# Layer 1 of a two-layer graph attention network: the tile's last two neighbouring multiplied rows are added on GpSimd first

## The chip, the cores and the metric

The kernel runs on one core of a Trainium2 chip. The metric is the device time of one execution in microseconds (us), from the first to the last instruction and what lies around them. Each execution computes the whole network from inputs in HBM. The engines are TensorE (PE, its weight loads PEld), VectorE (DVE), ScalarE (ACT), GpSimd (POOL) and SyncE (SP, which only issues DMAs here). Each engine works through its own list of instructions in order; semaphores hold an instruction until what it needs is done.

## What is computed

Two graph attention layers with a residual and a layer norm each, over 10000 nodes with 768 features and 170000 edges (self loops among them); the reference adds one more self loop to each node. All in float32. Cut to what matters for layer 1 (4 heads of 256 columns, 1024 in all):

```python
src, dst = ei[0], ei[1]
xl = (x @ W).reshape(n, heads, out_ch)
alpha_src = einsum('nhc,hc->nh', xl, a_src)
alpha_dst = einsum('nhc,hc->nh', xl, a_dst)
e = leaky_relu(alpha_src[src] + alpha_dst[dst], 0.2)
e = exp(e - segment_max(e, dst)[dst])
alpha = e / (segment_sum(e, dst)[dst] + 1e-16)
h = segment_sum(xl[src] * alpha[:, :, None], dst)   # the sum of this case
h = relu(layer_norm(h + b1)) + (x @ Wr1 + br1)
# layer 2 the same with one head of 768 columns, then
# x = layer_norm(x + layer 2 + its residual)
```

## The kernel before

**Stages.** First a table is made (to about 900 us): for each tile of 128 nodes `x @ W1` and the attention terms are written to a table in HBM, while the edges are sorted into lists. Then layer 1 runs (`ordered_layer1`, about 910 to 3350 us), then layer 2 (to the end).

**Tiles of layer 1.** The nodes are sorted by degree and cut into 79 tiles of 128 nodes, one node a partition. A tile `t` has `n = SLOTS[t]` rows: row `k` holds, for each of its 128 nodes, the table row of the node's k-th neighbour (1033 floats a partition). `n` goes from 8 up to 41 in the middle tile and down to 9; there are 1377 rows in all. The rows come by GpSimd's indirect DMAs (`gather`, L426) into a ring of 29 rows in SBUF (`Ring`, `RING1 = 29`). `ring.fetch(upto)` issues all gathers below `upto` that are not issued yet; it is called after each row, so the gather that reuses a row's place is queued on GpSimd right after the row was used, and waits for that use.

**The weighted sum of a tile** is made in `acc`, which lies in PSUM, from three kinds of rows:

- the first `on_pe(t)` rows (1 to 4) go through TensorE: ScalarE writes diagonal matrices of the weights (L725), TensorE multiplies the rows by them into `acc` (L731). In tiles of 22 rows and more, the later groups have such rows too;
- of the rest every fourth (`SHARE = 4`) is weighted by VectorE alone, `acc += weight * row`, four instructions of 256 columns (`weigh`, L531);
- all others are `shared`: ScalarE multiplies the row in place by its weights (`multiply`, L520, four instructions), `LEAD = 3` rows ahead in the program's order, and VectorE adds the whole row to `acc` (`weigh`, L527, one instruction of 1024 columns).

VectorE takes the rows in order, so `acc` is read and written by one instruction after the other.

**The next tile's weights** are prepared by VectorE in between. Before row `n - 3` it makes the logits of the next tile: L489 adds the attention terms in the ring's rows to `ad`, L190 is the leaky relu, L493 the largest, L496 the subtraction (about 1.05 us in all); ScalarE takes the exponential (L497). Before row `n - 2` VectorE normalises them: L514, L508, L509, L510, L511 (about 1.2 us). Then ScalarE writes the diagonals and TensorE starts the next tile's rows. In the text below the first of these is called the list step and the second the normalising step. All operands of both lie in SBUF. On GpSimd each list step has a few short instructions as well (L500, L501).

**The end of a tile** on VectorE is the layer norm: L542 and L544, L556, L558, L856 (about 5.7 us); its first weighted row of the next tile then waits until TensorE's L731 is complete. TensorE's order in a tile is: transposes of x (L697), transposes of `h` (L697), `x @ Wr1` (L173, 24 matmuls), the layer-2 table row (L879, 32 matmuls), then L731 of the next tile.

The schedule is written out by hand: each engine executes in the order in which the Python emits.

Of the kernel before, what the change touches and what calls it, by code (L numbers as in the profile page):

```python
# [48 lines left out]
LEAD = 3  # L49
# [3 lines left out]
ON_PE1 = 4  # L53
PARTED2 = 26
PARTED = 22


def chunk_counts(n_edges):
# [23 lines left out]
def gnn_kernel(ctx, tc, x, x_cols, src, dst, src_col, dst_col, W1, a_src1, a_dst1, b1, g1, be1, Wr1, br1,  # L82
               W2, a_src2, a_dst2, b2, g2, be2, Wr2, br2, out, n_edges):
    nc = tc.nc
    N, D0 = out.shape
    H1, DH1 = a_src1.shape
    H2, DH2 = a_src2.shape
    C1, C2 = H1 * DH1, H2 * DH2
# [8 lines left out]
    SLOTS = CAPS  # L97
# [3 lines left out]
    FIRST, TOTAL = [0] * NT, 0  # L101
# [420 lines left out]
    def weigh(acc, row, e, dh, first=None, shared=False):  # L522


        if shared:
            c = e.shape[1] * dh
            nc.vector.tensor_add(acc[:, :c], acc[:, :c], row[:, :c])  # L527
            return
        for h in range(e.shape[1]):
            s = slice(h * dh, (h + 1) * dh)  # L530
            nc.vector.scalar_tensor_tensor(acc[:, s], row[:, s], e[:, h:h + 1],  # L531
                                           (acc if first is None else first)[:, s], op0=OP.mult, op1=OP.add)
# [110 lines left out]
    SLOTS, FIRST = [SLOTS[t] for t in TURNS], [FIRST[t] for t in TURNS]  # L643
# [31 lines left out]
    def ordered_layer1(mem):  # L675
        nc.scalar.add_instruction(mybir.InstLoadActFuncSet(name=nc.get_next_instruction_name(), act_func_set_id=6, engine=nc.scalar.engine))
        with tc.tile_pool(name="b1", bufs=1) as pool, tc.tile_pool(name="small1", bufs=2) as small, \
# [3 lines left out]
            ring = Ring(table1, RING1, {}, [mem.rearrange("p (k n) -> p k n", n=R1)])  # L681
# [30 lines left out]
            def on_pe(t):  # L712


                return min(max(SLOTS[t] // 2 - 5, 1), ON_PE1, SLOTS[t])

            def later_on_pe(t):

                return min(max((SLOTS[t] - 20) // 2, 1), ON_PE1)
# [61 lines left out]
            def cuts_of(t):  # L781

                n = SLOTS[t]
                groups = 1 if n < PARTED else -(-2 * n // ring.size)
                size = 8 if groups == 2 else (n - 5) // groups
                return [0] + [n - size * g for g in range(groups - 1, -1, -1)]

            def by_vector(t, k):
                lo = max(c for c in cuts_of(t)[:-1] if c <= k)
                return k - lo >= (later_on_pe(t) if lo else on_pe(t))  # L790

            def shared(t, k):
                return by_vector(t, k) and (k - on_pe(t)) % SHARE > 0

            last = None
            full = None
            ready = []
# [18 lines left out]
            for t in range(NT + 1):  # L816
                live, events = t < NT, []
                n = SLOTS[t] if live else 0
                first = done = on_pe(t) if live else 0
                cuts = cuts_of(t) if live else []  # L820
                if live and not ready:
# [3 lines left out]
                def row_of(k):  # L825
                    lo = max(c for c in es if c <= k)
                    return es[lo][0][:, k - lo], es[lo][1] if k == lo else None

                def multiplied(upto):
                    nonlocal done  # L830
                    while done < min(upto, n):
                        if shared(t, done):
                            multiply(ring.slot(FIRST[t] + done), row_of(done)[0], DH1)
                        done += 1
# [5 lines left out]
                if live:  # L840
                    es, acc = ready
# [52 lines left out]
                def due(k):  # L894
                    while events and events[0][0] <= k:
                        events.pop(0)[1]()
# [5 lines left out]
                for k in range(n):  # L902
                    if k + 2 * LEAD + 2 in cuts[1:-1]:
                        next(later)
                    if k + 2 * LEAD in cuts[1:-1]:
                        lo, es_lo = next(later)
                        es[lo] = es_lo
                    multiplied(k + 1 + LEAD)
                    if n - LEAD <= k < n - LEAD + 2:
                        ready += itertools.islice(ahead, 1)  # L910
                    if k + 2 in cuts[1:-1]:
                        next(later)
                    weights, fade = row_of(k)
                    if fade is not None:
                        for h in range(H1):
                            s = slice(h * DH1, (h + 1) * DH1)
                            nc.vector.scalar_tensor_tensor(acc[:, s], acc[:, s], fade[:, h:h + 1], ring.slot(FIRST[t] + k)[:, s],
                                                           op0=OP.mult, op1=OP.add)
                    if by_vector(t, k):
                        weigh(acc, ring.slot(FIRST[t] + k), weights, DH1, shared=shared(t, k))  # L920
                    ring.fetch(FIRST[t] + k + 1 + ring.size)
                    due(k)
                due(DEGREES)
                ready += itertools.islice(ahead, max(2 - len(ready), 0))
# [409 lines left out]
    with tc.If(all_fits > 0) as fit:  # L1334
        with tc.tile_pool(name="rows", bufs=1) as rows_pool:
            mem = rows_pool.tile([P, RING1 * R1], F32, name="ring")
            ordered_layer2(mem, ordered_layer1(mem))
# [49 lines left out]
```

## Time and profile before

| | us |
|---|---|
| median of 3 runs | 5521.68 |
| lowest and highest | 5516.3 and 5529.82 |
| the profiled execution | 5544.64 |
| its span, first to last instruction | 5542.8 |
| busy in the span: PE, DVE | 4908.0, 4286.7 |
| busy in the span: ACT, POOL | 2828.9, 3296.8 |
| in layer 1: 807 adds of a shared row (L527) | 993.8 |
| in layer 1: 1248 weighted quarter rows (L531) | 610.9 |
| in layer 1: 1361 gathers on POOL (L426) | 1389.0 |

The last three are from the groups of instructions between 913 and 3350 us. The profile has one record of each instruction: engine, line, start, duration, and what ended the idle time before it. "a<-b,c" names what is written and what is read. Busy time is not a bound by itself: which engine sets the pace has to be read from the waits of each stage.

### The profile page before, as it was taken

To read this page: it belongs to the slowest core of one execution; us is meant where nothing else is said; L and a number is where in the kernel's file an instruction comes from. 1 tells how busy PE (TensorE), PEld (TensorE's weight loads), DVE (VectorE), ACT (ScalarE), POOL (GpSimd) and SP (SyncE) were. 2 spreads that over 40 slices of the span, in tenths; PEclk is the share of its full clock that TensorE was granted. 3 is DMA by queue.
4 is the path that set the end of the run, shared out by engine and by line. 5 is a ranking of instruction groups with operands and counts; after the bars stand their busy time and mean duration, and the time that the engine had idled before them with its cause. 6 is when DMAs were issued, how large, how long until landed. Compare 5 with 4: busy or idle time off the path is not lost. (4 is left out here: it accounts for less than half of the span.)

```text
span 5542.8 us, 60338 instructions
## 1 busy us (share of the span) xinstructions
PE 4908.0 (89%) x15304; PEld 2913.5 (53%) x15307; DVE 4286.7 (77%) x7678; ACT 2828.9 (51%) x8248; POOL 3296.8 (59%) x3429
## 2 busy tenths in 40 slices
PE   8999996999999887889999997999888887877765
PEld 3444443555555555555655554666555555555544
DVE  5883244899998888899999995988777776766776
ACT  3434343777778788778777772332322222222222
POOL 2446365556666666666666544666665665666663
PEclk9999997999999999999999998999998988888887
DMA  4333626899999998999999977999988888888885
GB/s 156 122 96 88 94 91 236 312 344 354 363 376 363 356 348 292 342 348 369 374 365 358 341 272 263 333 331 333 329 313 286 301 304 291 291 290 289 298 291 184
DMA packets 474313, 1591.43 MB, mean 287 GB/s; under 512 B 118328, under 2 KB 122488, under 8 KB 473959
## 3 DMA queue, kind: packets, MB, share of 16 engines
q0 software_dynamic: 322384, 1286.62, 65.5%
q1 hardware_dynamic: 149520, 297.43, 16.1%
q10 hardware_dynamic: 2054, 3.42, 0.2%
q8 instruction: 129, 2.11, 0.2%
q14 instruction: 226, 1.84, 0.1%
HBM read 1431.80 MB, written 177.29 MB: 290 GB/s over the span
## 5 line engine op out<-in xcount | busy, mean ns | idle before, releaser
L426 POOL DMA_INDIRECT ring<-table,slots x2675 | 2658.3, 994 | 1633.8 <-issue 616.4
L531 DVE SCALAR_TENSOR_TENSOR acc<-ring,e,acc 128x256 f32<-128x256 f32 (+1 forms) x2546 | 1586.7, 623 | 141.6 <-PE acc L731 44.0
L520 ACT ACTIVATE ring<-ring,e 128x256 f32<-128x256 f32 x3232 | 1320.8, 508 | 1.4 <-issue 1.3
L527 DVE TENSOR_TENSOR acc<-acc,ring 128x1024 f32<-128x1024 f32 x808 | 995.1, 1232 | 78.1 <-remote 5.5
L1033 PE MATMUL big<-wr,w 128*128 128x512 f32 (+1 forms) x2464 | 875.8, 501 | 142.1 <-issue 138.2
L988 PE MATMUL big<-ring,diagonals 128*128 128x256 f32 x2754 | 750.4, 431 | 197.5 <-issue 149.1
L173 PE MATMUL big<-w,xT 128*128 128x512 f32 x1896 | 824.7, 597 | 26.3 <-DMA w<-in_W_dram 9.8
L173 PE MATMUL big<-wr,xT 128*128 128x512 f32 x1896 | 832.6, 596 | 0.2 <-ACT xT L698 0.2
L879 PE MATMUL half<-w,hT 128*128 128x512 f32 (+1 forms) x2528 | 830.5, 486 | 0.0
L988 PEld LDWEIGHTS big<-ring,diagonals 128*128 128x128 f32 x2754 | 590.4, 218 | 360.9 <-issue 226.9
L1033 PEld LDWEIGHTS big<-wr,w 128*128 128x128 f32 x2464 | 482.2, 196 | 503.6 <-issue 471.9
L987 ACT ACTIVATE diagonals<-ident,e 128x128 f32<-128x128 f32 x1377 | 423.1, 388 | 609.8 <-remote 228.6
L879 PEld LDWEIGHTS half<-w,hT 128*128 128x128 f32 x2528 | 477.7, 189 | 367.8 <-issue 330.8
L731 PE MATMUL acc<-ring,diagonals 128*128 128x256 f32 x2056 | 514.3, 406 | 138.2 <-ACT diagonals L725 99.5
L173 PEld LDWEIGHTS big<-w,xT 128*128 128x128 f32 x1896 | 361.7, 191 | 484.9 <-issue 466.9
L173 PEld LDWEIGHTS big<-wr,xT 128*128 128x128 f32 x1896 | 356.4, 191 | 419.9 <-issue 419.2
L731 PEld LDWEIGHTS acc<-ring,diagonals 128*128 128x128 f32 x2056 | 411.0, 203 | 237.8 <-ACT diagonals L725 125.2
L546 ACT ACTIVATE sd<-mv,eps 128x1 f32<-128x1 f32 x237 | 69.3, 292 | 690.2 <-DVE mv L544 426.5
L725 ACT ACTIVATE diagonals<-ident,e 128x128 f32<-128x128 f32 x1028 | 315.4, 388 | 173.2 <-DVE e L511 115.8
L630 DVE TENSOR_TENSOR scr<-big,ad_b 128x1024 f32<-128x1024 f32 x79 | 96.7, 1225 | 377.5 <-ACT row L627 337.7
L635 POOL TENSOR_TENSOR row<-row,none 128x1024 f32<-128x1024 f32 x79 | 187.2, 2369 | 264.0 <-ACT row L627 261.4
L633 ACT ACTIVATE scr<-scr 128x256 f32<-128x256 f32 x632 | 253.5, 402 | 120.3 <-DVE scr L630 120.3
(185 smaller groups left out, 3453.5 us busy)
## 6 DMA issues: line engine op xcount, KB each, us to landing
ring<-table,slots POOLq DMA_INDIRECT x2675
table<-row SPq DMA_DIRECT2D x79, 516.0 KB
h_d<-hT SPq DMA_DIRECT2D x79, 512.0 KB
w<-h_d SPq DMA_DIRECT2D x77, 512.0 KB
table<-row SPq DMA_DIRECT2D x79, 385.0 KB
ring<-table SPq DMA_DIRECT2D x79, 385.0 KB
xT<-in_x_cols_dram SPq DMA_DIRECT2D x79, 384.0 KB
x_d<-xt SPq DMA_DIRECT2D x79, 384.0 KB
```

The costliest lines, as they stand in the source:

```text
L173: nc.tensor.matmul(p[:, c:e], aT[:, j, :], w[:, j, c:e], start=(j == 0), stop=(j == k - 1))
L426: nc.gpsimd.indirect_dma_start(out=to, out_offset=None, in_=table, in_offset=bass.IndirectOffsetOnAxis(ap=index, axis=0), **more)
L520: nc.scalar.activation(row[:, s], row[:, s], AF.Copy, scale=e[:, h:h + 1])
L527: nc.vector.tensor_add(acc[:, :c], acc[:, :c], row[:, :c])
L531: nc.vector.scalar_tensor_tensor(acc[:, s], row[:, s], e[:, h:h + 1], (acc if first is None else first)[:, s], op0=OP.mult, op1=OP.add)
L633: nc.scalar.activation(m[:, s], m[:, s], AF.Copy, accum_out=row[:, C1 + i * H1 + h:C1 + i * H1 + h + 1])
L725: nc.scalar.activation(diagonals[:, k * H1 + i, :], ident, AF.Copy, scale=e[:, k, i:i + 1])
L731: nc.tensor.matmul(acc[:, c:d], diagonals[:, k * H1 + i, :], ring.slot(q + k)[:, c:d], start=(k == 0 and c % BANK == 0), stop=(k == m - 1 ...
L879: nc.tensor.matmul(q, hT[:, j, :], w2[:, j, c:c + q.shape[1]], start=(j == 0), stop=(j == K1 - 1))
L987: nc.scalar.activation(diagonals[:, (k - lo) % G, :], ident, AF.Copy, scale=e[:, k - lo, :])
L988: nc.tensor.matmul(to, diagonals[:, (k - lo) % G, :], ring.slot(at + k)[:, ON_PE2:C2], start=False, stop=(k == n - 1), skip_group_check=True)
L1033: nc.tensor.matmul(r[:, c:d], hT[:, j, :], wr2[:, j, c:d], start=False, stop=(j == K1 - 1 and d < C2), skip_group_check=True)
```

## The change

In tiles of at least 14 rows two neighbouring shared rows, `pair` and `pair + 1`, the last such two in the tile's last group, are not added to `acc` one by one. GpSimd adds the first to the second in place in the ring, and VectorE adds that sum to `acc` as the tile's last row. The fetches that reuse the places of row `pair` and all later rows of the tile are put off to the tile's end.

```diff
+PAIRED = 14
...
+            def pair_of(t):
+
+                n, lo = SLOTS[t], cuts_of(t)[-2]
+                for k in range(n - 2 if n >= PAIRED else -1, lo, -1):
+                    if shared(t, k) and shared(t, k + 1):
+                        return k
+                return n
...
+                pair = pair_of(t) if live else 0
...
+                    if k == max(pair + 1 - LEAD, n - 5) and pair < n:
+                        one, two = (ring.slot(FIRST[t] + pair + j)[:, :C1] for j in (0, 1))
+                        nc.gpsimd.tensor_add(two, two, one)
                     weights, fade = row_of(k)
...
-                    if by_vector(t, k):
+                    if by_vector(t, k) and k not in (pair, pair + 1):
                         weigh(acc, ring.slot(FIRST[t] + k), weights, DH1, shared=shared(t, k))
-                    ring.fetch(FIRST[t] + k + 1 + ring.size)
+                    if pair < n and k == n - 1:
+                        weigh(acc, ring.slot(FIRST[t] + pair + 1), weights, DH1, shared=True)
+                        pair = n
+                    ring.fetch(FIRST[t] + min(k + 1, pair) + ring.size)
                     due(k)
```

By the code, 65 of the 79 tiles have a pair. Rows are numbered from 0; the list step stands before row n - 3, the normalising step before row n - 2. GpSimd's add is queued after the gather that follows the row in the third column:

| rows n | tiles | last row before the add | pair | order on VectorE from there, after the change |
|---|---|---|---|---|
| 14 | 6 | 9 | 12, 13 | row 10, list, 11, normalise, sum |
| 15 | 8 | 9 | 12, 13 | 10, 11, list, normalise, 14, sum |
| 16 | 7 | 10 | 13, 14 | 11, 12, list, normalise, 15, sum |
| 17 | 8 | 11 | 13, 14 | 12, list, normalise, 15, 16, sum |
| 18 | 7 | 12 | 14, 15 | 13, list, normalise, 16, 17, sum |
| 19 | 7 | 14 | 17, 18 | 15, list, 16, normalise, sum |
| 20 | 6 | 15 | 18, 19 | 16, list, 17, normalise, sum |
| 21 | 4 | 15 | 18, 19 | 16, 17, list, normalise, 20, sum |
| 22 | 4 | 16 | 18, 19 | 17, list, normalise, 20, 21, sum |
| 23 | 2 | 18 | 21, 22 | 19, list, 20, normalise, sum |
| 24 to 41 | 6 | | | as one or the other of these |

## The prediction

> **What bounds layer 1 now.** I read the groups of instructions first, for the prices of the two adds: VectorE's add of a shared row into PSUM, and the only large add that GpSimd does in this kernel, of the same size, in the table stage. The number after the bar is busy us, the next the mean ns of one.
>
> ```profile
> L527 DVE TENSOR_TENSOR acc<-acc,ring 128x1024 f32<-128x1024 f32 x808 | 995.1, 1232 | 78.1 <-remote 5.5
> L635 POOL TENSOR_TENSOR row<-row,none 128x1024 f32<-128x1024 f32 x79 | 187.2, 2369 | 264.0 <-ACT row L627 261.4
> ```
>
> Next the busy time by windows, cut at tile borders (from one L542 to the next): tiles of 15, 16, 17 and 19 rows. Columns: window, length, then busy us of PE, PEld, DVE, ACT and POOL, clock, DMA.
>
> ```profile
> 1226.20:1253.90 27.70, 25.91 (x88) 15.17 (x87) 25.83 (x41) 20.02 (x53) 16.76 (x20) 1.00 0.95 348
> 1337.00:1365.00 28.00, 27.54 (x96) 16.57 (x95) 26.02 (x41) 21.30 (x57) 17.75 (x21) 1.00 0.99 369
> 1451.50:1480.60 29.10, 27.78 (x95) 16.46 (x95) 27.11 (x42) 22.79 (x61) 19.40 (x20) 1.00 0.99 369
> 1631.40:1662.60 31.20, 29.85 (x104) 17.98 (x103) 28.55 (x43) 25.55 (x70) 21.60 (x25) 1.00 1.00 379
> ```
>
> Two engines are full at once. VectorE's missing 2 us are gaps of some 0.05 us between its 40 instructions; TensorE misses 0.5 us (16 rows) to 1.8 us (15). GpSimd has 8 to 11 us free. So VectorE's row is worth its 1.25 us only where TensorE leaves room for it, and from 19 rows on there is a third limit, seen in the timeline of one 19-row tile (start, duration; VectorE, then GpSimd, ScalarE, TensorE):
>
> ```profile
> 1653.37 2.57 DVE L527 TENSOR_TENSOR acc<-acc,ring 128x1024 f32<-128x1024 f32 x2
> 1655.85 0.30 DVE L489 TENSOR_TENSOR e<-ring 128x4 f32<-128x4 f32 x2
> 1656.18 0.30 DVE L190 SCALAR_TENSOR_TENSOR e<-e 128x76 f32<-128x76 f32 x1
> 1656.84 0.24 DVE L496 TENSOR_TENSOR e<-e,new 128x76 f32<-128x76 f32 x1
> 1656.99 2.06 DVE L531 SCALAR_TENSOR_TENSOR acc<-ring,e,acc 128x256 f32<-128x256 f32 x4
> 1659.96 0.24 DVE L511 TENSOR_TENSOR e<-e,total 128x76 f32<-128x76 f32 x1
> 1660.11 2.49 DVE L527 TENSOR_TENSOR acc<-acc,ring 128x1024 f32<-128x1024 f32 x2
> ```
>
> ```profile
> 1654.88 0.99 POOL L426 DMA_INDIRECT ring<-table,slots  x1 [0.35 <-issue]
> 1656.21 0.99 POOL L426 DMA_INDIRECT ring<-table,slots  x1 [0.34 <-issue]
> ```
>
> ```profile
> 1660.29 2.44 ACT L725 ACTIVATE diagonals<-ident,e 128x128 f32<-128x128 f32 x8 [2.91 <-DVE e L511]
> 1660.74 3.72 PE L731 MATMUL acc<-ring,diagonals 128*128 128x256 f32 x16 [0.26 <-ACT diagonals L725]
> ```
>
> The list step (L489 to L496) leads through the normalising step (to L511) and the diagonals to TensorE, which waits for them, and VectorE waits for TensorE at its next first row: in the waits of this tile DVE L531 <- PE L731 is 0.6 us, PE L731 <- ACT L725 0.9 us. So from 19 rows on the list step is on the path that sets the tile's length, and the rows after L511 (the two of 1660.11, which are the pair here) are not. GpSimd is in step with VectorE: its gather starts 0.27 us after the row before it ended (1654.61, the first of the two L527).
>
> **The part that hurts.** GpSimd's add falls exactly there. Last, a place where such an add met VectorE, in the table stage: the answer for L278, VectorE's short add with both inputs in SBUF, and the timeline where it met L635; then L630, VectorE's product with one input in PSUM, which runs beside L635 all the time.
>
> ```profile
> L278 DVE TENSOR_TENSOR before<-before,hot x79: 182/192/2272, 382.9 to 408.9; 128x64 bf16<-128x64 bf16 x79
> 382.94 2.38 POOL L635 TENSOR_TENSOR row<-row,none 128x1024 f32<-128x1024 f32 x1 [7.93 <-ACT row L627]
> 382.91 3.36 DVE L278 TENSOR_TENSOR before<-before,hot 128x64 bf16<-128x64 bf16 x6
> L630 DVE TENSOR_TENSOR scr<-big,ad_b x79: 1212/1225/1226, 24.1 to 877.9; 128x1024 f32<-128x1024 f32 x79
> ```
>
> Minimum, median and maximum in ns: 192 as a rule, 2272 at worst. Six of them at 382.91 took 3.36 us instead of 1.35: one was held until the GpSimd add had ended. It happened in both of the two places where an L278 started under an L635. L630 never went over 1226.
>
> **The change, part by part.** *VectorE's add removed*: 65 tiles with one L527 less, 1.25 us with its gap: 65 x 1.25 = 81 us at most. *ScalarE's multiplications*: unchanged. *Fetches put off*: the gathers for the last 2 to 4 places of a tile are issued at its end instead; the next tile's rows (n' of them) need places up to row n + n' - 30 of this one, which is below the pair in every tile, and GpSimd's free 8 to 11 us take them: 0; if that cover were gone, the list step would wait for a late row, at most 1.7 us in the waits between 1500 and 3360 us. *GpSimd's add*: 65 x 2.37 us, beside other work on GpSimd (19.40 + 2.37 of 29.10 us); behind it in the queue stand the next gather and the short L500 and L501, nobody near waits for them. Its wait for ScalarE's second product is over by 1.3 us after the last row before it (I call that row's end T0) in tiles of 17 to 19 rows, at about 1.5 us with 20 and 21, at 1.2 to 2.8 us in the small ones. VectorE needs the sum at T0 + 6 us or later in tiles of up to 23 rows: no wait.
>
> *The block.* No row shows the list step under such an add. Bounds: nothing, as L630, or until the add ends, as L278. L489, L190, L496 and L511 have both inputs in SBUF, so L278 is the nearer row and I take the full block. The adds of rows into `acc` (PSUM) go as L630. With the gather at T0 + 0.27 and 0.99 us long, the add runs from T0 + 1.33 to T0 + 3.70, later where ScalarE is late. Per tile:
>
> - 17, 18 and 22 rows: one row is gone before the list step, which now starts at T0 + 1.25 (before: 2.58), its first instruction slips through, the rest waits to 3.7 and ends at 4.65. The exponential, hidden behind a row before, shows 0.35 us (its 0.27 and gaps); the normalising step ends at 6.05 (before, at 1451 to 1480 us: 5.88), then come three rows instead of two: VectorE is 1.4 us later. 17 rows: 8 x 1.4 = 11.2. With 18 and 22 rows VectorE had 0.57 us of waiting for TensorE: 11 x 0.85 = 9.4.
> - 19 and 23 rows: nothing is removed before the list step; it starts at 1.25, waits to 3.7, less its first 0.25: the chain to TensorE is 2.2 us later, and the row saved lies behind it: 9 x 2.2 = 19.8.
> - 20 rows: list step at 2.0, add to 3.9; it ends at 4.95 instead of 3.58 (the mean start of the next row in the six tiles, DMA waits included): 6 x 1.4 = 8.4.
> - 14 and 16 rows: ScalarE's product is there only at 2.4 to 2.8, the add ends near 5.1. 16 rows: list step at 3.35 held 1.75 us, a row saved behind it less 0.35 us of exponential: +0.85. 14 rows: L496 held 2.2 us, a row saved: +1.0, of which 0.3 us falls into a wait. 13 x 0.8 = 10.4.
> - 15 and 21 rows: list step at 3.35, add to about 4.0: 0.7 us held, 0.9 us saved: 12 x -0.1 = -1.
> - 24 to 41 rows: GpSimd is 2 to 4 us behind in some, the block falls elsewhere: -0.75 to +1.1 each; I take +1 in all.
>
> Sum: 11.2 + 9.4 + 19.8 + 8.4 + 10.4 - 1 + 1 = **+59 us**. The profiled execution took 5544.64 us (1.84 around the span), 0.4% above the median of the runs; against it 5604, against the median **5580 us**.
>
> The Trainium skill, SBUF — State Buffer, section "SBUF: two separate sides", says that VectorE and GpSimd share a port pair as an exclusive lock for a whole instruction, and that a VectorE instruction with two SBUF inputs takes it against a GpSimd instruction that reads SBUF. The trace agrees with L278's 2272 ns against L635. By the rule the sum is the +59 us above; if the row held only for 16-bit adds such as L278, it would be the -28 us of the first rival.
>
> **Rivals.**
> *Faster, the list step isn't held.* For it: L630 runs beside L635, and L278 is a 16-bit add. Then 17-row and 15-row tiles save 1.25 - 0.35 = 0.9 us less small losses, 0.8 x 16; 14, 16 and 18 rows 0.3 x 20 (TensorE has only 0.5 us room); 19, 20 and 23 nothing; 21 and 22 0.8 x 8; the rest 3 in all: -28 us, 5494. It decides where the hold is worth less than 28 / 65 = 0.43 us a tile. Against it: the held L278 twice of two.
> *No difference.* The hold falls into slack of VectorE (0.57 us of waits in most tiles from 18 rows on) and into DMA waits that the list step had anyway, and the saved row pays the rest: 5522. Against it: in the tiles of 16 and 17 rows the waits show no slack.
> *Much slower.* GpSimd falls behind, rows land late, and the list step waits 1.7 us more in each of the 65 tiles: 110 us on top, 5690. Against it: GpSimd's 8 to 11 free us a tile.
>
> **How the numbers follow.** Forecast 0.72, faster 0.10, none 0.10, much slower 0.08. The predicted time is the forecast's, 5580; its own bounds are 30 us either way (the class prices are from one tile each). What a measurement can tell from no change is 0.3%, 5505 to 5538. Below it: the faster rival and a hundredth, 0.11; within it: 0.10 and the forecast's lower edge, 0.13; above: 0.76. The range of 8 in 10 leaves most of the faster rival and of the worst one out: 5510 to 5625.
>
> **What would show it.** Right: L489, L190 or L496 with maxima near 2.4 us, ending with GpSimd's add; 743 L527 instead of 808; GpSimd's add at 2.37 us; longer waits of TensorE for diagonals in 19-row tiles, which grow from 31.2 to some 33.4 us, while 15-row tiles stay at 27.7. Wrong: list instructions at their old 0.2 to 0.3 us; a GpSimd add that starts after L496; a VectorE wait for GpSimd before the last L527; L489 waiting for DMA.

## The result and the profile after

The changed kernel took **5653.86 us** (median of 4 runs, 5647.21 to 5658.24) against 5520.73 us of the kernel before (4 runs): a ratio of **1.0239** (95% interval 1.0220 to 1.0257), 133 us more. Its profiled execution took 5656.21 us, its span was 5654.4 us, the mean granted clock of TensorE 0.933 (before: 0.940). From its first layer norm to its last (lines L542, L543) layer 1 takes 2551.0 us instead of 2416.4, 134.6 us more: all of the 133 us are there. (The two profiled executions are only 112 us apart, because that of before spent 2191.5 us behind layer 1, the other 2170.4.) The lines of the changed kernel up to L793 stand one further down: L489 is now L490, L190 is L191, L496 is L497, L511 is L512, L514 is L515, L527 is L528, L531 is L532, L725 is L726, L731 is L732.

The groups of instructions that answer to those shown of before, and TensorE's of before with them (after the bar: busy us, mean ns of one, then idle us before them and what ended it):

```profile
L528 DVE TENSOR_TENSOR acc<-acc,ring 128x1024 f32<-128x1024 f32 x743 | 915.4, 1232 | 119.6 <-ACT ring L521 39.6
L731 PE MATMUL acc<-ring,diagonals 128*128 128x256 f32 x2056 | 514.3, 406 | 138.2 <-ACT diagonals L725 99.5 <-issue 33.8 <-ACT ring L520 2.8
L732 PE MATMUL acc<-ring,diagonals 128*128 128x256 f32 x2056 | 549.1, 427 | 218.0 <-ACT diagonals L726 161.9
```

VectorE's adds went from 808 to 743 at the same 1232 ns: 80 us of its work are gone. But TensorE now waits 161.9 us for diagonals instead of 99.5, and its matmuls into `acc` last 427 ns on average instead of 406: the granted clock stands at one half for 256 us of layer 1 (40 stretches) instead of 171 us (22). The same windows as before, tiles of 15, 16, 17 and 19 rows:

```profile
1227.50:1255.00 27.50, 25.64 (x87) 14.93 (x86) 25.25 (x40) 20.01 (x53) 19.07 (x21) 1.00 0.97 351
1339.40:1367.80 28.40, 27.63 (x96) 16.64 (x96) 26.10 (x41) 21.18 (x57) 20.14 (x22) 1.00 0.97 358
1458.50:1489.50 31.00, 28.68 (x100) 17.25 (x98) 28.09 (x40) 22.79 (x61) 20.82 (x21) 1.00 0.93 340
1658.40:1693.00 34.60, 31.29 (x103) 19.23 (x102) 29.53 (x42) 25.67 (x70) 23.80 (x26) 0.94 0.95 341
```

In the 17-row tile VectorE is busy for 28.09 us with 40 records, where it was busy for 27.11 with 42: less work takes longer. Why is in the durations of the list step (minimum, median, maximum in ns), first before:

```profile
L489 DVE TENSOR_TENSOR e<-ring x99: 154/196/258, 909.8 to 3325.3; 128x40 f32<-128x40 f32 x9, 128x36 f32<-128x36 f32 x9, 128x32 f32<-128x32 f32 x7, 128x24 f32<-128x24 f32 x7
L190 DVE SCALAR_TENSOR_TENSOR e<-e x174: 168/192/302, 910.0 to 5507.1; 128x32 f32<-128x32 f32 x12, 128x56 f32<-128x56 f32 x10, 128x60 f32<-128x60 f32 x10, 128x68 f32<-128x68 f32 x10
L496 DVE TENSOR_TENSOR e<-e,new x174: 167/194/295, 910.5 to 5507.7; 128x32 f32<-128x32 f32 x12, 128x56 f32<-128x56 f32 x10, 128x60 f32<-128x60 f32 x10, 128x68 f32<-128x68 f32 x10
```

Then after:

```profile
L490 DVE TENSOR_TENSOR e<-ring x99: 149/216/3043, 909.0 to 3457.9; 128x40 f32<-128x40 f32 x9, 128x36 f32<-128x36 f32 x9, 128x32 f32<-128x32 f32 x7, 128x24 f32<-128x24 f32 x7
L191 DVE SCALAR_TENSOR_TENSOR e<-e x174: 168/193/3157, 909.2 to 5618.4; 128x32 f32<-128x32 f32 x12, 128x56 f32<-128x56 f32 x10, 128x60 f32<-128x60 f32 x10, 128x68 f32<-128x68 f32 x10
L497 DVE TENSOR_TENSOR e<-e,new x174: 168/193/3041, 909.7 to 5619.0; 128x32 f32<-128x32 f32 x12, 128x56 f32<-128x56 f32 x10, 128x60 f32<-128x60 f32 x10, 128x68 f32<-128x68 f32 x10
L515 DVE TENSOR_SCALAR e<-e,loops x158: 206/214/2352, 910.2 to 5597.5; 128x4 f32<-128x4 f32 x79, 128x1 f32<-128x1 f32 x79
L925 POOL TENSOR_TENSOR ring<-ring x65: 2343/2355/2448, 1112.7 to 3310.4; 128x1024 f32<-128x1024 f32 x65
L745 DVE COPY ad<-ring x12: 159/1508/2440, 1935.7 to 2438.2; 128x4 f32<-128x4 f32 x12
```

The medians of the first four are nearly as before, maxima are 2.4 to 3.2 us, where none of these lines went over 0.31 us before. In one 19-row tile (VectorE, GpSimd, then ScalarE and TensorE):

```profile
1685.30 2.57 DVE L490 TENSOR_TENSOR e<-ring 128x4 f32<-128x4 f32 x2
1687.90 0.24 DVE L191 SCALAR_TENSOR_TENSOR e<-e 128x76 f32<-128x76 f32 x1
...
1685.34 2.35 POOL L925 TENSOR_TENSOR ring<-ring 128x1024 f32<-128x1024 f32 x1
...
1691.94 1.28 ACT L726 ACTIVATE diagonals<-ident,e 128x128 f32<-128x128 f32 x4 [2.91 <-DVE e L512]
...
1692.40 1.17 PE L732 MATMUL acc<-ring,diagonals 128*128 128x256 f32 x2 [2.85 <-ACT diagonals L726]
```

L490 began at 1685.30, GpSimd's add ended at 1687.69, and only then the list step went on; TensorE, which had waited 0.6 to 1.2 us for the diagonals in such tiles, waited 2.85 us. From here on I call *held* what an instruction of the list or the normalising step (L490, L191, L494, L496, L497, L512, L515) takes beyond the median of its line, where it takes over 600 ns, summed over layer 1. Before: 0. After: 99.6 us, under 55 of the 65 adds, one instruction under each, and each of the 55 ended 0.03 to 0.11 us after the add did. One line is missing from this sum: in tiles of 22 rows and more the list step begins with a copy of four numbers out of a ring row (L745; L744 before, where it took 0.42 us at most). Seven of these copies lasted until the add ended, 13.8 us more, so that the change held 113.4 us under 62 of its 65 adds.

A second loss was not in any step of mine: ScalarE's copies of `hT` (the transposed `h`, which TensorE leaves in PSUM) wait for TensorE. The waits of the changed kernel (us in total, times, longest):

```profile
ACT hT L699 <- remote: 27.9, 10, 4.4
ACT hT L699 <- PE big L174: 10.8, 4, 5.0
```

The trace of before has none over 0.1 us, this one 15, 39.5 us together. In the first 18-row tile:

```profile
1527.71 3.30 ACT L521 ACTIVATE ring<-ring,e 128x256 f32<-128x256 f32 x8
1531.70 0.58 ACT L699 COPY hT<-half 128x512 f32<-128x512 f32 x1 [0.69 <-PE big L174]
1536.68 0.58 ACT L699 COPY hT<-half 128x512 f32<-128x512 f32 x1 [4.39 <-remote]
...
1538.89 1.23 DVE L528 TENSOR_TENSOR acc<-acc,ring 128x1024 f32<-128x1024 f32 x1 [4.39 <-ACT ring L521]
```

The transposes that these copies wait for have records that end at 1528.5, yet TensorE's signal came 3 and 8 us later; the multiplications queued behind the copy on ScalarE were late in turn, and VectorE stood for 4.39 us.

### The profile page after: what moved, and what is told of

The parts are those of the page before. It is cut to its first block, busy times and chain, and to the rows that moved or that the text cites. A ratio compares the mean times of both kernels' runs of the same rounds, so it can differ in the third digit from the quotient of the medians.

```text
span 5654.4 us, 60306 instructions
## 1 busy us (share of the span) xinstructions
PE 4933.1 (87%) x15307; PEld 2935.1 (52%) x15307; DVE 4327.0 (77%) x7613; ACT 2831.9 (50%) x8248; POOL 3428.4 (61%) x3494
## 5 line engine op out<-in xcount | busy, mean ns | idle before, releaser
L532 DVE SCALAR_TENSOR_TENSOR acc<-ring,e,acc 128x256 f32<-128x256 f32 (+1 forms) x2546 | 1586.6, 623 | 175.8 <-PE acc L732 79.4
L521 ACT ACTIVATE ring<-ring,e 128x256 f32<-128x256 f32 x3232 | 1319.9, 505 | 0.0
L528 DVE TENSOR_TENSOR acc<-acc,ring 128x1024 f32<-128x1024 f32 x743 | 915.4, 1232 | 119.6 <-ACT ring L521 39.6
L732 PE MATMUL acc<-ring,diagonals 128*128 128x256 f32 x2056 | 549.1, 427 | 218.0 <-ACT diagonals L726 161.9
L732 PEld LDWEIGHTS acc<-ring,diagonals 128*128 128x128 f32 x2056 | 438.7, 217 | 325.1 <-ACT diagonals L726 185.0
L726 ACT ACTIVATE diagonals<-ident,e 128x128 f32<-128x128 f32 x1028 | 315.2, 387 | 150.6 <-DVE e L512 117.6
```

Source lines behind the costliest of these rows:

```text
L521: nc.scalar.activation(row[:, s], row[:, s], AF.Copy, scale=e[:, h:h + 1])
L726: nc.scalar.activation(diagonals[:, k * H1 + i, :], ident, AF.Copy, scale=e[:, k, i:i + 1])
L732: nc.tensor.matmul(acc[:, c:d], diagonals[:, k * H1 + i, :], ring.slot(q + k)[:, c:d], start=(k == 0 and c % BANK == 0), stop=(k == m - 1 ...
```

## The experiments

They ran on several chips, and these are of two sorts: in the experiments from e1_hold to e5_split the kernel before took 5517 to 5521 us, as in the comparison above, in the later ones 5182 to 5183 us, mostly because layer 2 is faster there (from the last layer norm of layer 1 to the end 1849 to 1854 us in the traces, against 2164 to 2192). The kernel before has no trace there. Every ratio is against the kernel before on the same chip. I call these the first and the second sort of chip. The diffs are against the changed kernel unless they say otherwise.

| kernel | GpSimd's add | chip | time, us | ratio (95%) | held, us (adds) | late hT, us |
|---|---|---|---|---|---|---|
| the change | pair, 2.36 us | first | 5653.86 | 1.0239 (1.0220 to 1.0257) | 99.6 (55) | 39.5 |
| e1_hold | idle row, 1.90 us | first | 5584.83 | 1.0106 (1.0074 to 1.0138) | 47.5 (40) | 0 |
| e2_defer | none | first | 5517.08 | 0.9994 (0.9980 to 1.0008) | 0 | 0.5 |
| e3_mid | pair in mid-tile | first | 5561.35 | 1.0075 (1.0051 to 1.0098) | 0 | 2.9 |
| e4_norm | pair, queued later | first | 5666.68 | 1.0263 (1.0231 to 1.0295) | 75.0 (35) | 17.0 |
| f1_idle | idle row, 1.90 us | first | 5597.23 | 1.0145 (1.0116 to 1.0175) | 72.5 (40) | 0 |
| f2_skip | none | first | 5513.90 | 0.9991 (0.9979 to 1.0002) | 0 | 4.4 |
| f6_burst | none | first | 5542.95 | 1.0044 (1.0029 to 1.0060) | 0 | 0.9 |
| e5_split | pair, four pieces | first | 5610.20 | 1.0172 (1.0144 to 1.0200) | 51.6 (89) | 24.3 |
| g1_idle2 | idle rows, 2.36 us | second | 5280.88 | 1.0189 (1.0172 to 1.0206) | 95.9 (50) | 0 |
| g2_half | pair, into an idle row | second | 5269.37 | 1.0169 (1.0152 to 1.0186) | 101.7 (53) | 0 |
| after_again | the change | second | 5277.74 | 1.0185 (1.0168 to 1.0202) | 104.1 (55) | 0 |
| g3_tiny | pair, 8 columns | second | 5163.18 | 0.9962 (0.9948 to 0.9977) | 0 | 0 |
| h1_gated | after the normalising step | second | 5228.48 | 1.0093 (1.0076 to 1.0110) | 0 | 0 |
| h2_small | the same, 14 to 18 rows | second | 5169.08 | 0.9973 (0.9964 to 0.9982) | 0 | 0 |

(Copies by L745 are not in the column of held: they add 6.4 us in e1_hold, 10.4 in f1_idle, 0.5 in e5_split, 13.1 in g1_idle2 and g2_half, 13.6 in after_again and after_b. For e5_split the number of adds is that of its 260 pieces. The runs after_b, g1_b, g1_c and g2_b repeat three of these on the second chip: 1.0185, 1.0191, 1.0187 and 1.0169.)

**e1_hold: the hold alone.** The kernel before, with an add on GpSimd at the change's place.

```diff
+                    if k == max(pair + 1 - LEAD, n - 5) and pair < n:
+                        idle = ring.slot(FIRST[t + 1] + 6)[:, :C1]
+                        nc.gpsimd.tensor_add(idle, idle, idle)
```

> The kernel before, and one GpSimd add of 128x1024 queued where the change has it, in 65 tiles; VectorE adds all rows at their old places, no fetch is put off. (The add doubles row 6 of the next tile in place, so that row counts twice in the result.) Theory H, GpSimd's add holds VectorE's list step: nothing is saved and the list step starts one row later than in the change in 17-, 18- and 22-row tiles, so it is held 1.1 us there, 2.2 in 14-, 19- and 23-row tiles, 1.4 to 1.8 in 16- and 20-row tiles, 0.6 in 15- and 21-row tiles: 60 to 110 us slower than before, 5580 to 5630, with L190 or L496 up to some 2.4 us. Theory Q, the loss comes from the fetches that are put off: no more than 20 us slower, list instructions at 0.2 to 0.3 us.

5584.83 us: the hold by itself costs 64 us, near the lower end. Row 6 of each next tile is counted twice here. What I had not seen then: a row added to itself takes GpSimd 1.90 us, not 2.36, so this is a mild form of the hold.

**e2_defer: the put-off fetches alone.**

```diff
-                    if k == max(pair + 1 - LEAD, n - 5) and pair < n:
-                        one, two = (ring.slot(FIRST[t] + pair + j)[:, :C1] for j in (0, 1))
-                        nc.gpsimd.tensor_add(two, two, one)
...
-                    if by_vector(t, k) and k not in (pair, pair + 1):
+                    if by_vector(t, k):
...
-                        weigh(acc, ring.slot(FIRST[t] + pair + 1), weights, DH1, shared=True)
```

> The kernel before with only the change's put-off fetches (the gathers for the places of row pair and later rows of a tile are issued at its end); no GpSimd add, VectorE adds all rows. Theory H: within 0.3% of before, 5505 to 5538. Theory Q: most of the 133 us, and in particular the waits of ScalarE's copies of hT for TensorE (4.4 us each, only in the changed kernel, mostly in 18-row tiles): 40 us or more slower, 5560 and up, with those waits in the trace.

0.9994: the put-off fetches cost nothing, and that rival is out.

**e3_mid: the pair in the middle of the tile**, far from the list step, tiles of 14 to 21 rows.

```diff
-                n, lo = SLOTS[t], cuts_of(t)[-2]
-                for k in range(n - 2 if n >= PAIRED else -1, lo, -1):
-                    if shared(t, k) and shared(t, k + 1):
-                        return k
-                return n
+                n, k = SLOTS[t], on_pe(t) + SHARE + 1
+                return k if n >= PAIRED and n < PARTED else n
...
-                    if k == max(pair + 1 - LEAD, n - 5) and pair < n:
+                    if k == pair - 1 and pair < n:
...
-                    if pair < n and k == n - 1:
+                    if pair < n and k == pair + 3:
```

> The change with another pair: the sixth and seventh row after TensorE's rows, in tiles of 14 to 21 rows (53 tiles), added by GpSimd while VectorE adds rows to PSUM, the sum added three rows later, before the list step; fetches are put off by at most three rows. Theory H: nothing with two SBUF inputs is near, so no hold; VectorE and the list step are 1.25 us earlier, of which TensorE leaves 0.2 to 0.5 us in 14-, 16- and 18-row tiles and nearly all in the others: 30 to 50 us faster than before, 5470 to 5490. Theory Q: the put-off fetches and GpSimd's 2.4 us in its queue still cost: no faster than before, 5520 or more.

A miss: nothing is held, as it should be, but the time is 1.0075. The wait that took its place, in the waits and in the timeline of an 18-row tile of this kernel:

```profile
DVE acc L528 <- ACT ring L521: 107.1, 59, 5.6
...
1562.52 1.23 DVE L528 TENSOR_TENSOR acc<-acc,ring 128x1024 f32<-128x1024 f32 x1 [1.71 <-ACT ring L521]
```

ScalarE multiplies a row in four pieces of 0.41 us (1320.8 us for 3232 before), 1.6 us a row, and is only some rows ahead there. Having skipped two rows, VectorE catches up with it and waits: 107 us, where the kernel before waited 2.2 us.

**e4_norm: the same pair, the add queued after the normalising step in the program's order.**

```diff
-                    if k == max(pair + 1 - LEAD, n - 5) and pair < n:
+                    if k == n - LEAD + 1 and pair < n:
```

> The change with GpSimd's add queued after the normalising step instead of before the list step; the same pair, the same put-off fetches, the sum last. Theory H: the list step keeps 0.2 to 0.3 us an instruction; the price is a wait of VectorE for the sum, about 2.4 us in 14-, 19-, 20- and 23-row tiles, 0.5 in 15-, 16- and 21-row tiles, none in 17-, 18- and 22-row tiles, which gain: 0 to 40 us slower than before, 5520 to 5560, clearly faster than the change. Theory Q: as slow as the change, 5630 to 5670.

A miss, and an instructive one. A later place in the program is not a later start: the gathers that would have made GpSimd wait for VectorE are put off in the change, so its queue runs ahead, and the add starts beside the normalising step instead (VectorE, GpSimd):

```profile
1488.52 2.33 DVE L515 TENSOR_SCALAR e<-e,loops 128x4 f32<-128x4 f32 x1 [1.93 <-ACT e L498]
...
1488.48 2.35 POOL L925 TENSOR_TENSOR ring<-ring 128x1024 f32<-128x1024 f32 x1 [0.97 <-ACT e L498]
```

L512 (up to 3.20 us) and L515 (2.33 us) are held now, 75 us in all, and L510, a tensor with a constant, six times, 12 us more. To the rest of its 146 us belongs the wait that the expectation had named: VectorE stands for the sum, as the waits say,

```profile
DVE acc L528 <- POOL ring L925: 45.4, 19, 5.0
```

and there are late `hT` copies (17 us) and other late signals: above, both engines wait for the exponential, whose record ended 1.4 us earlier.

**f1_idle, f2_skip: the skipped row with and without an add.** In f1_idle the add of e1_hold takes the place of the change's, in f2_skip there is none.

```diff
-                        one, two = (ring.slot(FIRST[t] + pair + j)[:, :C1] for j in (0, 1))
-                        nc.gpsimd.tensor_add(two, two, one)
+                        idle = ring.slot(FIRST[t + 1] + 6)[:, :C1]
+                        nc.gpsimd.tensor_add(idle, idle, idle)
```

> The changed kernel with the GpSimd add on a row of the ring that lies idle (a row of the next tile) instead of on the pair: same place in GpSimd's queue, same length, same put-off fetches, VectorE skips the first row of the pair and adds the second one last. The first row of each pair is left out of the sum, and the idle row is doubled. What is gone: GpSimd's wait for ScalarE's products, and VectorE's wait for GpSimd. W (what the change costs beyond the hold of 58 us comes from that chain ScalarE, GpSimd, VectorE): 5520 to 5590, no late hT copies of ScalarE. S (it comes from VectorE reaching the list step a row earlier): 5640 to 5660, as the changed kernel. B (GpSimd's block, its wait and its add together, bunches the fetches, and in the bunch TensorE's signals come late): 5580 to 5630, late copies in fewer tiles.

> The changed kernel without any GpSimd add: VectorE skips the first row of each pair, which is left out of the sum, and adds the second one last; put-off fetches as in the change. It gives what the removed VectorE instruction is worth by itself, 65 x 1.25 = 81 us at most. W and B: 5490 to 5521, because TensorE has only 0.5 us free in the tiles of 13 to 18 rows. S: above 5560.

f2_skip says what the saved instruction is worth on the first sort of chip when nothing is held: 3 us of the 81, not to be told from no change. S is out with that: a list step that comes a row earlier costs nothing by itself. f1_idle takes 83 us more than f2_skip, for 72.5 us held. That is above W's range, since VectorE, a row earlier at the list step, stands longer under the add than in e1_hold (47.5 us); it lies in B's, but without the late copies that B asks for. The timeline of a 17-row tile of f1_idle:

```profile
1444.43 0.29 DVE L490 TENSOR_TENSOR e<-ring 128x44 f32<-128x44 f32 x2
1444.76 2.57 DVE L191 SCALAR_TENSOR_TENSOR e<-e 128x68 f32<-128x68 f32 x1
...
1444.31 0.99 POOL L427 DMA_INDIRECT ring<-table,slots  x1 [0.30 <-issue]
1445.33 1.90 POOL L925 TENSOR_TENSOR ring<-ring 128x1024 f32<-128x1024 f32 x1
```

L191 began 0.57 us before the add's record does, under the gather ahead of it, and should have been over at 1444.98. It ended with the add all the same. In f1_idle, where the add's record always follows a gather's within 0.1 us, this befell all 16 instructions of L490, L191 and L497 that began 0.22 to 0.72 us ahead of the add, and all 17 in g1_idle2. In the change's trace it befell 6 of 8 such (up to 0.70 us ahead), but none of the 13 for which GpSimd stood idle ahead of the add, waiting for ScalarE. So a short instruction just ahead of the add slips through where GpSimd is idle, and hardly where a gather runs right up to the add.

**f6_burst: the fetches for the last six rows put off, no add.** Against the kernel before:

```diff
-                    ring.fetch(FIRST[t] + k + 1 + ring.size)
+                    far = n if n < PAIRED or k == n - 1 else n - 6
+                    ring.fetch(FIRST[t] + min(k + 1, far) + ring.size)
```

> The kernel before, with the fetches for the last six rows of each tile from 14 rows on put off to the tile's end, so that they come in a bunch; no add on GpSimd, nothing left out. B: ScalarE's hT copies wait for TensorE by 3 to 5 us in some tiles, 5540 or more. W and S: no such wait; 5515 to 5535.

The time fits B, the reason doesn't: 26 us more, but one late copy of 0.9 us. A bunch of fetches alone does not make TensorE's signals late. Six put-off rows do cost something, unlike the change's two to four.

**e5_split: the add in four pieces.**

```diff
-                        nc.gpsimd.tensor_add(two, two, one)
+                        for h in range(H1):
+                            s = slice(h * DH1, (h + 1) * DH1)
+                            nc.gpsimd.tensor_add(two[:, s], two[:, s], one[:, s])
```

> The changed kernel with the GpSimd add cut into four of 256 columns. If the hold lasts for one GpSimd instruction: a list instruction waits at most some 0.6 us at a time, the list step runs between the pieces, maxima of L490, L191 and L497 below 1.2 us, 5570 to 5630. If it lasts until GpSimd's queue is empty: maxima near 2.4 us or above and 5650 or more.

1.0172. In the timeline of a 17-row tile the list step moves on between the pieces (VectorE, GpSimd):

```profile
1476.58 0.67 DVE L490 TENSOR_TENSOR e<-ring 128x68 f32<-128x68 f32 x1
1477.29 0.65 DVE L191 SCALAR_TENSOR_TENSOR e<-e 128x68 f32<-128x68 f32 x1
...
1477.10 2.79 POOL L927 TENSOR_TENSOR ring<-ring 128x256 f32<-128x256 f32 x4
```

So the hold is mostly that of one GpSimd instruction, and the time is in the range that goes with it. But 8 of the 93 held instructions took 1.5 to 2.92 us, two pieces or more, against the 1.2 us that I had expected at most; why these did not get in between is open.

**g1_idle2, g2_half, after_again: full length, with and without the waits.** g1_idle2 adds two idle rows (2.36 us); g2_half adds the pair, as soon as ScalarE has both, into an idle row, so that VectorE need not wait for it.

```diff
-                        one, two = (ring.slot(FIRST[t] + pair + j)[:, :C1] for j in (0, 1))
+                        one, two = (ring.slot(FIRST[t + 1] + 6 + j)[:, :C1] for j in (0, 1))
```

```diff
-                        nc.gpsimd.tensor_add(two, two, one)
+                        idle = ring.slot(FIRST[t + 1] + 6)[:, :C1]
+                        nc.gpsimd.tensor_add(idle, two, one)
```

> As f1_idle (the add on rows that lie idle, VectorE skips the first row of each pair, which is left out of the sum), but the add takes two different idle rows, so that it lasts 2.36 us as in the change, where e1_hold and f1_idle, which added a row to itself, had 1.90 us. Nothing waits for ScalarE or for GpSimd. If the time is the hold's: 65 adds x up to 0.46 us more, some 45 of which meet the list step: 20 us over f1_idle, 5610 to 5625. If the length of the add does not matter: 5590 to 5600. What is left to the changed kernel's 5654 then belongs to its waits.

> As the change, but the sum of the pair goes into a row that lies idle, and VectorE adds the second row of the pair last as ScalarE left it (the first row of each pair is left out). GpSimd's add still waits for ScalarE's two products, so it starts when it does in the change; VectorE doesn't wait for GpSimd. If the waiting of GpSimd (a later start, hence more of it on the list step, and a later bunch of fetches) makes the rest: 5640 to 5660, with late hT copies. If VectorE's wait for the sum makes it: the same as g1_idle2, without late copies.

> The changed kernel once more, for a second trace: 5640 to 5665. If the late hT copies hang on the program's order they are in the same tiles (three of the 18-row tiles in a row among them) with some 40 us in all; if they are chance, in others, with the time moving with their sum.

On this sort of chip the change costs 96 us, not 133, and an add that waits for nobody and for which nobody waits costs as much: 1.0189 against 1.0185. The length of the add counts (f1_idle, 1.90 us: 1.0145, on the other sort). GpSimd's wait for ScalarE costs nothing to be seen here. g2_half, where VectorE waits for no sum and the sum is written elsewhere, is 8 to 11 us faster than the change both times it ran, every run of it below every run of the change; which of the two differences does it was not tried. And no `hT` copy is late in any of the three, nor in their repeats; the tiles of 18 rows take 31.9 to 32.3 us on average in the change, where its first trace had 35.07. So the late copies do not follow from the program's order alone; and the four runs of the change on the first sort of chip, 5647 to 5658 us, speak against chance in the one traced. Four kernels were run once more side by side, to see whether the waits bring them on a chip of the first sort:

> The changed kernel a third time. Where the kernel before takes some 5520 us on the chip: 5645 to 5665, ScalarE's hT copies late by 30 to 50 us in all; where it takes some 5180 us: ratio 1.0185, none late. In both, list step and normalising step held by some 100 us in all.

> The add on two idle rows once more, beside the changed kernel on this chip. Ratio 1.0185 to 1.02 wherever it runs, no late copies, if the hold is all of it and the late copies need the waits of the change; the ratio of the changed kernel, with late copies, if a 2.36 us add by itself brings them on a chip where the kernel before takes 5520 us.

> GpSimd waiting for ScalarE's products, VectorE not waiting for GpSimd, once more. On a chip where the kernel before takes 5520 us: late copies and 1.024 if GpSimd's wait brings them; none and 1.017 to 1.02 if it takes VectorE's wait for the sum.

They met the second sort again (before: 5183.41 us), as did g1_c later, and only repeat what stands above: the question stays open.

> The add on two idle rows a third time. Where the kernel before takes some 5520 us: late hT copies and a ratio near 1.024 if any 2.36 us add at that place brings them; none and about 1.019 if they need the waits of the change. Where it takes some 5180 us: 1.019 again, none late.

**g3_tiny: all of the change but the length of the add.** As g2_half, with 8 columns:

```diff
-                        one, two = (ring.slot(FIRST[t] + pair + j)[:, :C1] for j in (0, 1))
-                        idle = ring.slot(FIRST[t + 1] + 6)[:, :C1]
+                        one, two = (ring.slot(FIRST[t] + pair + j)[:, :8] for j in (0, 1))
+                        idle = ring.slot(FIRST[t + 1] + 6)[:, :8]
```

> As g2_half with an add of 8 columns instead of 1024: GpSimd waits for ScalarE's products as in the change and the fetches behind it are as late, but it holds nothing for long. The first row of each pair is left out of the sum, and 8 columns of an idle row are overwritten. The hold's account: no list instruction above 0.5 us, 0.998 to 1.001. If GpSimd's wait alone brings the late copies: they are there, and 1.005 to 1.01.

0.9962, better than expected: on the second sort of chip the saved row is worth 20 us. Against it the full-length add costs 117 us in the changed kernel (after_b, 5280.48 us), for 117.5 us held (103.9 and 13.6 in L745).

**h1_gated, h2_small: keep the saved row, lose the hold.** The pair lies some rows earlier, and a copy of four numbers that the normalising step writes stands ahead of the add in GpSimd's queue, so that it can't start sooner. h2_small has `n <= 18` for `n < PARTED`.

```diff
-                for k in range(n - 2 if n >= PAIRED else -1, lo, -1):
+                for k in range(n - 4 if PAIRED <= n < PARTED else -1, lo, -1):
...
-                    if k == max(pair + 1 - LEAD, n - 5) and pair < n:
+                    if k == n - 2 and pair < n:
+                        if ready:
+                            gate = small.tile([P, H1], F32, name="gate")
+                            nc.gpsimd.tensor_copy(gate, ready[0][0][0][:, 0])
```

> A version meant to keep the saved row and lose the hold: in tiles of 14 to 21 rows (52 of the 65) the pair lies a few rows earlier, and GpSimd's add is made to wait for the next tile's normalising step, by a copy of four of its numbers ahead of it in the queue, so that it meets only VectorE's rows into PSUM, two of which still stand before the sum. If the hold is what costs: list and normalising steps at their 0.2 to 0.3 us, and the worth of the saved row: 0.996 to 1.000 of the time before. If the fetches put off for up to six rows cost as in f6_burst, or VectorE waits for the sum by more than the row saved: 1.000 to 1.008.

> As h1_gated, with the pairs only in the tiles of 14 to 18 rows (36 tiles), where the fetches put off for up to six rows were not missed: in h1_gated these tiles took 25.96, 27.11, 27.75, 28.48 and 29.73 us on average, by rows, against 25.93, 27.86, 27.83, 29.19 and 29.97 in the kernel before. 6 x 0 + 8 x 0.75 + 7 x 0.08 + 8 x 0.71 + 7 x 0.24 = 14 us: 0.9973 of the time before, no list or normalising instruction above 0.5 us, no wait of the list step for DMA in these tiles. If the gain of one trace was chance, or the next tiles give it back: 0.999 to 1.001.

h1_gated holds nothing, and yet takes 1.0093. (Its trace has 53 adds, not 52.) What L490 waited for in it, over the whole kernel:

```profile
  DMA ring<-table,slots: 224.0, 70
```

Of this, 72 us lie in tiles of 19 to 21 rows (5 us in h2_small): in most of them the list step waits 2 to 7.6 us for rows whose fetches were put off too long (20 rows: 37.36 us instead of 33.24). In the paired tiles of up to 18 rows there is only one such wait above 0.4 us, of 1.6 us, and h2_small keeps to them: **0.9973 (0.9964 to 0.9982)**, 14 us less than before, as worked out from h1_gated's tiles. It is faster than both kernels, 0.3% faster than the kernel before; it ran on the second sort of chip alone. A 17-row tile of it, in the windows and in the timeline (VectorE, GpSimd):

```profile
1437.50:1465.90 28.40, 27.79 (x96) 16.79 (x95) 26.05 (x42) 22.79 (x61) 20.98 (x22) 1.00 1.00 390
```

```profile
1458.63 0.22 DVE L490 TENSOR_TENSOR e<-ring 128x68 f32<-128x68 f32 x1
...
1461.05 0.23 DVE L512 TENSOR_TENSOR e<-e,total 128x68 f32<-128x68 f32 x1
1461.19 2.06 DVE L532 SCALAR_TENSOR_TENSOR acc<-ring,e,acc 128x256 f32<-128x256 f32 x4
1463.28 2.57 DVE L528 TENSOR_TENSOR acc<-acc,ring 128x1024 f32<-128x1024 f32 x2
...
1461.34 0.18 POOL L926 COPY gate<-e 128x4 f32<-128x4 f32 x1 [0.75 <-DVE e L512]
1461.50 2.35 POOL L928 TENSOR_TENSOR ring<-ring 128x1024 f32<-128x1024 f32 x1
```

The add of 1461.50 runs beside L532 and L528, which write `acc` in PSUM and are not slowed. It is over at 1463.85, and the second L528 is the sum.

## Why the prediction failed

The direction and the mechanism were right, the size was not: 59 us forecast, 133 measured, outside the stated range of 5510 to 5625 us. By tile, in us for all tiles of a class. The first sort is the change's first trace against that of before. The second sort is after_again, against the trace of before for 14 to 18 rows and against h2_small, on the same sort and without pairs there, for the others; it is an estimate, but its sum is the 96 us measured.

| rows | forecast | first sort | second sort |
|---|---|---|---|
| 17 | 11.2 | 14.5 | 14.5 |
| 14 and 16 | 10.4 | 7.8 | 7.3 |
| 20 | 8.4 | 11.2 | 13.4 |
| 19 and 23 | 19.8 | 28.9 | 21.6 |
| 15 and 21 | -1 | 8.2 | 1.8 |
| **18 and 22** | **9.4** | **48.8** | **25.6** |
| **24 to 41** | **1** | **13.0** | **10.5** |
| below 14 | 0 | 2.1 | 1.9 |
| sum | 59 | 134.5 | 96.6 |

Three steps failed: the credit in tiles of 18 and 22 rows and the block in those of 24 and more, on both sorts of chip, and "ScalarE's multiplications: unchanged", with no wait of ScalarE in the sum, on the first.

- *18 and 22 rows: "VectorE is 1.4 us later", "VectorE had 0.57 us of waiting for TensorE", hence 0.85 a tile.* Both the saved row and this slack were set against the hold, and neither paid. In g3_tiny, on the second sort, with the row saved and nothing held, tiles of 18 rows take 29.90 us, as against 29.97 in the trace of before: the row is worth nothing there. And the slack was not used up: in the change's first trace and in after_again VectorE still waits for TensorE by 0.57 us or more in all seven tiles of 18 rows, as TensorE's diagonals come late behind the held list step. So most of the hold came through: in after_again 2.3 to 2.8 us were held in each tile of 18 rows and 2.4 lost on average (2.3 in those of 22).
- *24 to 41 rows: "the block falls elsewhere", +1 in all.* In five of the six tiles an instruction was held until the add ended, L490, L497, L515 or the copy of L745, at 1.98 to 2.90 us each.
- *The late `hT` copies.* They are a new wait of ScalarE for TensorE, 39.5 us by the waits, for which none of my steps had a place. The change's cost differs by 133 - 96 = 37 us between the two sorts of chip, and 33 of these lie in the tiles of 18, 21, 22 and 23 rows, where all late copies but one stand. That they make the difference is inferred from place and size; no run takes them away on the first sort.
- *The block, "I take the full block" by the nearer row L278.* Right. 55 of 65 adds hold an instruction of the list or normalising step until they end, L490, L191 and L497 go to 3 us, and the adds into PSUM never went over 1.23 us. Undoing it (g3_tiny) takes the loss away. The Trainium skill, SBUF — State Buffer, section "SBUF: two separate sides", has the rule that fits: an exclusive lock, held for a whole instruction. It also gives the pair to whichever instruction starts first, and with that the trace does not always agree: L191 at 1444.76 began 0.57 us before the add's record and lost, though the starts of GpSimd's records are rough.
- *"Its first instruction slips through"* (17, 18 and 22 rows). Right in five of the seven tiles of 18 rows in the change's first trace, where GpSimd stood idle ahead of the add; wrong in the two others, and in three of the four of 22 rows, where the copy of L745 is that first instruction.
- *The size of the block.* The forecast's +59 against the -28 of its first rival makes 87 us of block. Measured, 113.4 us were held, with the copies of L745. A held us costs about 1 us against the same kernel without the hold: 117.5 held cost 117 (after_b against g3_tiny), in f1_idle 82.9 cost 83 (against f2_skip); only e1_hold, at 53.9 held and 64 lost, is off that.
- *The credit for the saved row*, 28 us in the first rival, was too high for the first sort of chip, where f2_skip gives 3 us, and near for the second, where g3_tiny gives 20.
- *Costed at nothing*: the put-off fetches (e2_defer, 0.9994), ScalarE's multiplications themselves (1319.9 us after, 1320.8 before) and VectorE's wait for the sum (2.2 us, once) were right, and so was 2.37 us for the add (2.36).
- *What was to show it* came mostly as said: 743 adds, maxima of the list step above 2.4 us, longer waits for diagonals, tiles of 15 rows at 27.5 us (27.7 forecast); the 19-row tile went to 34.6, not 33.4.
- *The rivals.* "The list step isn't held" is out. "Much slower", rows landing late, did not happen in the change (the list step's waits for gathers, over the whole kernel, fell from 62.3 to 42.1 us), but its mechanism is real: it is what spoiled h1_gated, with six fetches put off.

**Open.** Why TensorE's signals came late. They were late only on chips of the first sort, with nothing of it in before, e1_hold and f1_idle, some 40 us in the change, 24 in e5_split, 17 in e4_norm, 2.9 in e3_mid, and 4.4 in f2_skip, which has no add at all. The kernels with most of it are those whose add waits for ScalarE, but g1_idle2 and g2_half, which would have told, met only chips of the second sort.

## What to carry to other kernels

Work given to GpSimd is not off VectorE's path because VectorE's queue is shorter: here a GpSimd add of 2.36 us in SBUF stopped VectorE's short instructions on SBUF until it ended, those with two inputs but also a copy (reductions and adds into PSUM went on), so place it where VectorE writes or reads PSUM, and fix its start by a dependence, since a later place in the program does not. Ask first what the saved instruction is worth with nothing in its place: 80 us of VectorE's work were worth 3 to 20 us, and the placed version won 14, on the sort of chip where it was 20. And put no more fetches off than the list steps behind them can miss.

## What the runs showed of the hardware that was not expected

- An instruction on VectorE that starts up to 0.7 us ahead of GpSimd's add, under a gather that runs right up to the add, is held until the add ends (16 of 16 in f1_idle, 6 of 8 in the change); with GpSimd idle in between, none of 13 was.
- Two inputs in SBUF are not needed: L515 (128x4, one tensor and a column of scalars) is held too, at 2.35 us, and so are L745, a copy of 128x4 (2.44 us), and, in e4_norm, L510, a tensor with a constant (2.31 us). L494, a reduction with one input, never was (at most 0.31 us).
- GpSimd adds a row of 128x1024 to itself in 1.90 us, two different rows in 2.36 us.
- The same kernel before takes 5517 to 5521 us on some chips and 5182 to 5183 us on others, and the change's cost differs with them (133 and 96 us).
- TensorE's signal came up to 9.5 us after the records of its transposes had ended, in layer 1's tiles on the first sort of chip.
